# Four residual convolution layers on one NeuronCore: work between the layers in another order

## The chip, the cores and the metric

The kernel runs on one core of a Trainium2 chip. The metric is the device time of one execution in microseconds (us). The time of the kernel before is the median of three runs. Beside these runs there is one execution recorded by the hardware profiler; all times of single instructions, waits and transfers come from it.

## The reference, cut to what matters

The input x has the shape (4, 16, 512, 512) in float32: B = 4 images, C = 16 channels, 512 rows, 512 columns. Four layers follow each other, and each adds to x the result of a convolution of the normalised x:

```python
def _gn(v, G=8, eps=1e-5):          # GroupNorm: 8 groups of 2 channels, per image
    g = v.reshape(B_, G, C_ // G, H_, W_)
    m = jnp.mean(g, axis=(2, 3, 4), keepdims=True)
    s = jnp.var(g, axis=(2, 3, 4), keepdims=True)
    return ((g - m) / jnp.sqrt(s + eps)).reshape(v.shape)

x = x + L0(_gn(x)); x = x + L1(_gn(x)); x = x + L2(_gn(x)); x = x + L3(_gn(x))
```

- Layer 0 takes the 16 channels as 16 frames of a film. Two blocks come after each other. In a block each frame and its two neighbours go through three 5x5 convolutions with dilation 1, 2 and 4 and reflected edges; their results are weighted, added, and go through tanh.
- Layer 1 divides by the greatest absolute value of its whole input over 128, rounds to whole numbers between -127 and 127, runs a 3x3 convolution from 16 to 16 channels with zero edges, and scales the result and adds a bias.
- Layer 2 is the mean over a window of 17 rows and 17 columns, for each channel alone, with zero edges.
- Layer 3 takes the Fourier transform of each plane (rfftn over rows and columns), runs a complex 3x3 convolution from 16 to 16 channels over the frequencies, adds a complex bias, and transforms back.

A layer's normalisation needs the statistics of the whole image that the layer before put out (and layer 1 the greatest value of all images). So little of a layer can begin before the one before has ended.

## The kernel before, in words

All five engines take part. TensorE (PE) does the convolutions as matmuls into PSUM. ScalarE (ACT) and VectorE (DVE) normalise, round, add and gather statistics. SyncE (SP) issues nearly all transfers, ScalarE some at the beginning, and GpSimd (POOL) adds a few sums over the partitions. An engine works through its own instructions in order; one that has to wait holds up all that stand behind it. In the main loops the order is written out by hand: the program's order is each engine's order (`manual_schedule`).

**Layer 0** is the class Layer0 (L121 to L777). Its work is cut into groups of four frames, four groups for each block and image, 32 groups in all. Each group has six slots p = 0 to 5, in `run` (L722): a slot issues one sixth of the group's matmuls (`products`, L506), gathers the sixth before (`gather`, L529), prepares the frames of the group to come (`early`, `late`, `fetch`), and at last hands the slot's transfers to SP (`transfers`, L204), each tied to one of the slot's matmuls so that they spread over it. Group -1 has slots without matmuls, in which the first frames are made ready.

Ahead of that, `first` (L268) asks for the first HELD = 6 frames of image 0, two halves of 512 KB each. `weights` (L153) loads the table of all taps (`l0_t`, 1008 KB, on ScalarE's queue), weights and adds them on VectorE, stores them to DRAM from ScalarE's queue, and works out the two biases from two further small loads (L186 to L189). `load_weights` (L192) then loads the six sets of weights from there, in 24 transfers on ScalarE's queue. After that come the statistics of the six frames on VectorE (`frame_stats`, L257: four `bn_stats` for each frame, one `bn_aggr` for each pair) and `finish_stats` (L227), in which GpSimd adds over the partitions, and `rstd_bias` (L799) takes the square root on ScalarE and ends with the scale and the bias of the three groups. Only then can a frame be normalised (`x_frame`, L389; its rows at the edges, the rims, are loaded by `load_rims`, L345, and normalised at L366 to L382). The statistics of frames 6 to 15 are spread over the slots by `rest_of_first` (L291): one frame for each slot, two for each from (-1, 4) on. Their halves are loaded into the pool `x`, which has six buffers and is shared with the frames themselves. The sum of the other images' statistics is done in other slots.

**Layer 1** (L860) works through 64 chunks u of 8 rows of all four images. A chunk is loaded three chunks ahead, `rounded` normalises and rounds it (ScalarE, then VectorE) into one of three tiles `l1q`, which have a zero column at either end, `products` runs 256 matmuls, and `write` scales (ScalarE) and takes statistics (VectorE `bn_stats`, 64 x 6 values for each image). Before the first chunk, VectorE builds the weights `l_wt` from `l1_w` (a memset, L896, six operations, L901, and two scaled ones, L903) and clears the three `l1q` (L909). At the end four `bn_aggr` (L1007) put the statistics of 64 chunks together, one for each image, and `by_group` and `rstd_bias` turn them into scale and bias.

**Layer 2** (L1028) works through 64 planes i (image, channel). Each is loaded whole (1024 KB), normalised on ScalarE (L1070), multiplied twice with a band matrix (L1052), added to x (L1092) and stored. Every 16 planes `group_stats` (L827) ends an image's statistics. After image 1 and at layer 3's start, `edges` (L1255) works out in four steps, one for each step of layer 2's loop, what layer 3 needs of the images' first and last rows; it loads column sums that layer 2 stored.

`layer3_weights` (L1154) runs between layers 1 and 2: SP loads 14 constants, VectorE derives layer 3's weights (L1184 to L1231). Two more constants, band and cs, are loaded by layer 2.

**Layer 3** (L1347) works through 64 blocks yb of 8 rows. For a block: `load` (four transfers of 256 KB), `fold` (VectorE, sums and differences of the halves, L1253), `normal` (ScalarE, L1405), `products` (VectorE, L1421 and L1425), `rows` and `spread` (the block's own weights, VectorE then ScalarE), `imaginary` (L1456), `turned` (transposes, L1490), `scalars`, `real`, `hilbert` (L1515) and `write` (L1534). Before the loop the first two blocks are brought under way, together with the edges of images 2 and 3.

Of the kernel before, what the change touches and what calls it, by code (L numbers as in the profile page):

```python
# [20 lines left out]
P = 128  # L21
B, C, H, W = 4, 16, 512, 512
NYB = H // 8
G = 8
# [96 lines left out]
class Layer0:  # L121
# [31 lines left out]
    def weights(self):  # L153
# [28 lines left out]

        self.biases = k.const.tile([P, 2], F32, name="l0bias")
# [84 lines left out]
    def first(self):  # L268

        self.mv0 = self.k.stats.tile([P, G, 2], F32, name="xmv0")  # L270
        self.held = {}
        for t in range(HELD):
            fr = self.free.pop()
            raws = [fr[:, 2 * W * h : 2 * W * h + 2 * W] for h in range(2)]
            for h in range(2):
                self.load_half(raws[h], 0, t, h)
            self.held[0, t] = fr, raws
        self.weights()
        for q in ORDER:
            self.load_weights(0, q)  # L280
        for t in range(HELD):
            self.frame_stats(t, self.held[0, t][1])
        self.free.append(self.held.pop((0, HELD - 1))[0])
        self.finish_stats(0, self.mv0[:, 0 : HELD // 2])
        self.ahead = []
# [5 lines left out]
    def rest_of_first(self, n, p):  # L291

        if n == -1 and p == 0:
            self.transfers()
            for t in (HELD, HELD + 1):
                self.load_ahead(t)
            self.transfers()
        for _ in range(1 if n < 0 and p < 4 else 2):
            if self.ahead:
                t, raws = self.ahead.pop(0)  # L300
                self.frame_stats(t, raws)
                self.load_ahead(t + 2)
                if t == C - 1:
                    self.finish_stats(0, self.mv0[:, HELD // 2 : G], HELD // 2)
# [131 lines left out]
    def fetch(self, gr, p):  # L436

        b, conv, g = gr["b"], gr["conv"], gr["g"]
        if g == 0:
            order = {0: (1, 2), 1: (4,), 2: (3,), 4: (5,)} if conv else {0: (1,), 1: (2,), 2: (4,), 3: (3,), 4: (5,)}  # L440
        else:
            order = {0: (2,), 1: (4,), 2: (3,), 4: (5,)} if conv else {0: (2,), 1: (4,), 2: (3,), 4: (5,)}
        for i in order.get(p, ()):
            if g == 3 and i == 5:
                continue
            t = 4 * g - 1 + i
            if conv:
# [3 lines left out]
            rim = self.load_rims(b, t0) if i < 3 else None  # L451
            raws = None if (b, t) in self.held else [self.load_x(b, t, h, "xr") for h in range(2)]
            self.later(1, partial(self.made, gr, i, t, t0, rim, raws))
# [268 lines left out]
    def run(self):  # L722
# [57 lines left out]
class Kernel:  # L780
# [79 lines left out]
    def layer1(self, x1, x2, gn):  # L860
        tc, nc = self.tc, self.nc
        scale, bias, amax = gn
        with ExitStack() as ctx:
# [4 lines left out]
            wrep = self.load(wpool, "l1_w")  # L868
# [25 lines left out]

            wt = wpool.tile([P, 2, 4, 2, C], F32, name="l1_wt")
            nc.vector.memset(wt, 0.0)  # L896
            for a, yo, dhs in ((0, 0, (0, 1)), (0, 1, (None, 0)), (1, 0, (2, None)), (1, 1, (1, 2))):
                o = wt[:, a, 0:3, yo, :]
                for y, d in enumerate(dhs):
                    if d is not None:  # L900
                        nc.vector.scalar_tensor_tensor(o, wrep[:, d], row[:, y : y + 1], o, ALU.mult, ALU.add)  # L901
# [6 lines left out]
            for q in qs:  # L908
                nc.vector.memset(q, 0.0)  # L909
# [70 lines left out]
            with tc.tile_pool(name="l1ps", bufs=2, space=PSUM) as psum, tc.manual_schedule():  # L980
# [7 lines left out]
                for u in range(NYB + 2):  # L988
# [13 lines left out]
                    last = ps  # L1002

            gps = ctx.enter_context(tc.tile_pool(name="l1gps", bufs=2, space=PSUM))
            mv = wpool.tile([P, B, 2], F32, name="l1mv")
            for b in range(B):
                nc.vector.bn_aggr(mv[:, b, :], st[b].rearrange("p u s -> p (u s)"))  # L1007
# [20 lines left out]
    def layer2(self, x2, x3, sums, gn, l3):  # L1028
        tc, nc = self.tc, self.nc
        res, under_way = [], []  # L1030
        with ExitStack() as ctx:
# [10 lines left out]
            band = self.load(wpool, "c_band")  # L1042
            cs = self.load(wpool, "c_cs")
# [76 lines left out]
            with tc.manual_schedule():  # L1120
# [5 lines left out]
                for i in range(n + 1):  # L1126
# [11 lines left out]
                    if i > 0 and i % C == 0:  # L1138
                        b = i // C - 1
# [14 lines left out]
    def layer3_weights(self, wpool):  # L1154

        nc = self.nc
        l3 = SimpleNamespace(pool=wpool)
# [13 lines left out]
        bb = self.load(wpool, "l3_b")  # L1171

# [61 lines left out]
        return l3  # L1234
# [20 lines left out]
    def edges(self, l3, q, gn, sums, tiles, ps_u, ps_s):  # L1255
# [8 lines left out]
        yield 1  # L1264

# [81 lines left out]
    def layer3(self, x3, sums, gn, l3, out):  # L1347
# [3 lines left out]
        with ExitStack() as ctx:  # L1351
# [196 lines left out]
            with tc.manual_schedule():  # L1548
                edge = self.edges(l3, 1, gn, sums, tiles, ps_u, ps_s)
                next(edge)  # L1550
                for yb in range(2):
                    load(yb)
# [4 lines left out]
                next(edge)  # L1557
# [19 lines left out]
                turned(0)  # L1577
                next(edge, None)
                scalars(0)
# [25 lines left out]
    def run(self):  # L1605
# [5 lines left out]
        gn2 = self.layer1(x1, x2, gn1)  # L1611
        with self.tc.tile_pool(name="l3w", bufs=1) as wpool:
            l3 = self.layer3_weights(wpool)
            gn3 = self.layer2(x2, x3, sums, gn2, l3)
            self.layer3(x3, sums, gn3, l3, self.out)
# [63 lines left out]
```

## Time and profile before

| | us |
|---|---|
| median of 3 runs (5329.09 to 5343.41) | 5341.05 |
| profiled execution | 5351.83 |
| its span | 5350.0 |
| granted TensorE clock in it | 0.98 |
| TensorE busy with matmuls | 5027.4 (94%) |
| VectorE busy | 4035.8 (75%) |
| ScalarE busy | 2488.7 (47%) |
| mean DMA throughput | 161 GB/s |

The stages, by TensorE's matmuls in the trace:

| stage | us |
|---|---|
| start, to the first matmul of layer 0 | 0 to 80.8 |
| layer 0 | 80.8 to 3035.3 |
| layer 1, from its first full chunk | 3078.0 to 3666.7 |
| layer 2 | 3696.2 to about 4338 |
| layer 3, from its even running | 4384.0 to 5350 |

How to read it: the profile's span runs from the first to the last instruction, and the execution's own time is 1.8 us longer. Line numbers (L954) are those of the kernel shown here. Busy shares are means over stages of different kinds. An entry such as "DVE l1q L909" names the engine, the tile that is written, and the line; "SPq" and "ACTq" is an engine issuing a transfer. The chain of work follows back from the last instruction: at each step to what released it.

### The profile page before, as it was taken

The numbers are of one execution on the slowest core, as the hardware profiler recorded it, in microseconds if no ns is written. First come the engines' busy times: TensorE is split into PE (matmuls) and PEld (weight loads), VectorE is DVE, ScalarE is ACT, GpSimd is POOL, SyncE is SP. The second block draws the span as 40 slices with busy tenths as digits, with TensorE's granted clock in tenths as the row PEclk, the third lists the DMA queues.
The fourth block names the chain that finished last, engine by engine and source line by source line (L and its number), as shares of the span: only waits on it lengthen the run. The fifth ranks groups of instructions, "written<-read, shape, count | busy, mean of one in ns | idle before, by whom it ended". The sixth has DMA issues, their size and how long they took to land.

```text
span 5350.0 us, 270373 instructions
## 1 busy us (share of the span) xinstructions
PE 5027.4 (94%) x125040; PEld 3635.9 (68%) x125040; DVE 4035.8 (75%) x4739; ACT 2488.7 (47%) x3951; POOL 6.1 (0%) x18
## 2 busy tenths in 40 slices
PE   3999998999999999989999799997999979999999
PEld 2876676766666756757767565555887857777776
DVE  7867989768988669897688855555555578888887
ACT  2543345533245533443123454453454546666665
POOL 0000000000000000000000000000000000000000
PEclk9999999999999999999999899998999989999999
DMA  5455554555555455543345477775666655555554
GB/s 193 143 146 154 144 153 146 160 143 140 143 151 169 143 157 138 157 125 117 105 129 149 126 219 228 227 232 189 223 223 199 220 149 148 148 145 144 148 142 122
DMA packets 444349, 861.22 MB, mean 161 GB/s; under 512 B 73553, under 2 KB 95697, under 8 KB 442961
## 3 DMA queue, kind: packets, MB, share of 16 engines
q1 hardware_dynamic: 415216, 797.62, 51.1%
q10 hardware_dynamic: 28000, 46.31, 2.7%
q8 instruction: 979, 16.04, 1.4%
q14 instruction: 154, 1.25, 0.1%
HBM read 503.74 MB, written 339.90 MB: 158 GB/s over the span
## 4 chain that ended last, share of the span: by engine, by line
PE 90%; DVE 5%; issue 2%; DMA 1%; ACT 1%; SPq 0%; ACTq 0%; DVEq 0%; POOL 0%
PE m L518 53%; PE l1p L957 10%; PE l2p L1052 7%; PE u L1515 5%; PE s L1456 4%; PE u L1456 4%; PE u L1478 2%; PE pt L1490 2%; DVE l2o L1092 2%; PE l2p L1103 1%; DVE st L1093 1%; PE pr L1500 0%; DVE xst L264 0%; DVE frame L434 0%; DVE xb L625 0%
## 5 line engine op out<-in xcount | busy, mean ns | idle before, releaser
L518 PE MATMUL m<-frame,l0w 32*32 32x512 f32 x86016 | 2869.2, 605 | 166.1 <-DVE frame L474 80.8
L518 PEld LDWEIGHTS m<-frame,l0w 32*32 32x32 f32 x86016 | 2060.0, 103 | 974.4 <-issue 374.0
L434 DVE SCALAR_TENSOR_TENSOR frame<-frame,frame 128x2376 f32<-128x2376 f32 x232 | 607.8, 2628 | 8.3 <-DMA xb<-in_x 0.3
L957 PE MATMUL l1p<-l1q,l_wt 32*32 32x512 f32 x12288 | 484.4, 601 | 71.0 <-DVE l1q L947 38.4
L957 PEld LDWEIGHTS l1p<-l1q,l_wt 32*32 32x32 f32 x12288 | 259.5, 103 | 241.1 <-issue 164.7
L1092 DVE TENSOR_TENSOR l2o<-l2x,l2p 128x512 f32<-128x512 f32 x256 | 172.8, 675 | 258.7 <-PE l2p L1052 258.7
L645 ACT ACTIVATE junk<-xb,neg 128x1024 f32<-128x1024 f32 x256 | 294.3, 1150 | 63.8 <-DMA l0w<-l0w 31.3
L1052 PEld LDWEIGHTS l2p<-k_c_band,l2y 128*128 128x128 f32 x2048 | 256.7, 190 | 75.4 <-issue 54.6
L1052 PE MATMUL l2p<-k_c_band,l2n 128*128 128x144 f32 (+1 forms) x2048 | 271.4, 293 | 25.2 <-ACT l2n L1070 17.4
L1052 PE MATMUL l2p<-k_c_band,l2y 128*128 128x144 f32 (+1 forms) x2048 | 284.2, 292 | 6.1
L1081 ACT COPY l2y<-l2p 128x512 f32<-128x512 f32 x256 | 150.0, 586 | 285.1 <-PE l2p L1052 285.1
L1052 PEld LDWEIGHTS l2p<-k_c_band,l2n 128*128 128x128 f32 x2048 | 264.9, 198 | 25.8 <-ACT l2n L1070 17.8
L974 DVE BATCH_NORM_STATS2 l1st<-l1o 128x6 f32<-128x512 f32 x256 | 158.3, 681 | 161.9 <-ACT l1o L972 161.9
L972 ACT ACTIVATE l1o<-l1p,k_l_bias,l_osc 128x1024 f32<-128x1024 f32 x128 | 147.3, 1201 | 249.3 <-PE l1p L957 243.4
L1515 PE MATMUL u<-k_c_hil,zt 128*128 128x128 f32 x2048 | 255.9, 278 | 0.0
L551 ACT COPY C<-m 128x1024 f32<-128x1024 f32 x64 | 61.6, 1014 | 393.6 <-PE m L518 312.7
L1515 PEld LDWEIGHTS u<-k_c_hil,zt 128*128 128x128 f32 x2048 | 238.4, 192 | 2.1 <-issue 0.8
L398 DVE STREAM_TRANSPOSE frame<-xp 128x1056 f32<-128x1056 f32 x128 | 162.7, 1281 | 101.6 <-ACT xp L372 101.6
L1491 ACT COPY zt<-pt 128x512 f32<-128x512 f32 x256 | 131.5, 600 | 211.4 <-PE pt L1490 211.4
L1421 DVE TENSOR_TENSOR xc<-l3n,k_c_tab 128x2048 f32<-128x2048 f32 x64 | 146.7, 2293 | 108.3 <-ACT l3n L1405 108.3
L1534 DVE SCALAR_TENSOR_TENSOR l3o<-u,l3t 128x256 f32<-128x256 f32 x512 | 192.2, 427 | 23.7 <-ACT l3t L1526 20.9
L957 PE MATMUL l1p<-l1x,l_wt 32*32 32x512 f32 x4088 | 197.8, 597 | 0.0
(303 smaller groups left out, 6372.3 us busy)
## 6 DMA issues: line engine op xcount, KB each, us to landing
y<-y SPq DMA_DIRECT2D x256, 264.0 KB
frame<-y SPq DMA_DIRECT2D x512, 132.0 KB
x<-l1o SPq DMA_DIRECT2D x256, 256.0 KB
l2x<-x SPq DMA_DIRECT2D x64, 1024.0 KB
x<-l2o SPq DMA_DIRECT2D x64, 1024.0 KB
l3x<-x SPq DMA_DIRECT2D x256, 256.0 KB
out<-l3o SPq DMA_DIRECT2D x256, 256.0 KB
l1x<-x SPq DMA_DIRECT2D x252, 256.0 KB
```

What stands on the lines that cost most here:

```text
L398: nc.vector.transpose(v[:, :, 4 + h : 68 : 2], xp)
L434: self.nc.vector.scalar_tensor_tensor(o, x, f, y, ALU.mult, ALU.add)
L518: ins = nc.tensor.matmul(ps[PX * j : PX * j + PX, i, :].rearrange("p (k r) -> p k r", r=64), w[rows, n], v[rows, k0 : k0 + 8, r0 : r0 + 64 ...
L645: nc.scalar.activation(junk, xs[h], f, bias=neg, accum_out=self.out_sums[n][:, 2 * t + h : 2 * t + h + 1])
L957: ins = nc.tensor.matmul(ps[32 * j : 32 * j + 32, b, :], wt[rows, a, d], qs[v % 3][rows, k, d : d + W] if d < 3 else raws[v][rows, k], sta ...
L974: nc.vector.bn_stats(st[b][:, u, :], o[:, b, :])
L1052: nc.tensor.matmul(ps[:, lo:hi], lhs[:, k, at : at + P], band[:, j : j + hi - lo], start=(k == 0), stop=(k == 3), skip_group_check=True,)
L1081: nc.scalar.copy(yts[i][:, wb, :], ps)
L1092: nc.vector.tensor_add(o[:, hb, :], xt[:, hb, :], ps)
L1456: nc.tensor.matmul(ps[b][32 * j : 32 * j + 32], f[rows, n, j, :], x[rows, j, :], start=(i == 0), stop=(i == 2 and tag == "s"), skip_group_ ...
L1515: nc.tensor.matmul(po[:, bass.ts(k, P)], zt[:, b, k ^ 1, :], hil[:, k, :], start=False, stop=(k == 3), skip_group_check=True,)
L1534: nc.vector.scalar_tensor_tensor(o[:, v].rearrange("p k u -> p u k"), po[:, HW:W].rearrange("p (u k) -> p u k", u=2), s, t.rearrange("p (u ...
```

## The change: what it does

In the beginning of layer 0:
- The weights of layer 1, as far as they don't depend on data, are built first of all (`layer1_weights`, on tiles of layer 0 that are still free) and stored to DRAM; layer 1 loads them.
- The statistics of frames 0 and 1 come ahead of `weights`, those of frames 2 to 5 after it and after the 24 weight loads are issued.
- The biases become a function of their own, `take_biases`, called in slot (-1, 3).
- The rims of the first frames are asked for ahead of the statistics.
- The statistics of frames 6 to 15 move to later slots: two frames in slots (-1, 5) and (0, 0), then one in each; `finish_stats` runs for them in two parts, once for groups 2 to 4 (frames 4 to 9) and once for groups 5 to 7 (frames 10 to 15), instead of once for groups 3 to 7; groups 0 to 2 are done at the start as before.

In layer 1: only the two edge columns of the `l1q` tiles are cleared; layer 3's constants are loaded at chunk 4 and its weights derived at chunk 12 (`layer3_weights` becomes a generator in a pool opened ahead of layer 1, and takes over band and cs); the statistics of chunks 0 to 59 are put together at chunk 61, those of the last four at the end, and joined by five small operations.

In layer 2: `group_stats` of an image runs one plane later; `edges` of images 0 and 1 yields once more between its loads and their use.

In layer 3: before the loop, the first block's rows are loaded ahead of the edges' sums, and its fold, normalisation, products and matmuls come ahead of the edges' steps and of the second block.

```diff
@@ first
+        self.k.layer1_weights(self.free[3])
+        for t in range(2):
+            self.frame_stats(t, self.held[0, t][1])
         self.weights()
         for q in ORDER:
             self.load_weights(0, q)
-        for t in range(HELD):
+        self.rims_ahead = {t0: self.load_rims(0, t0) for t0 in (0, 1)}
+        for t in range(2, HELD):
             self.frame_stats(t, self.held[0, t][1])
@@ rest_of_first
-        if n == -1 and p == 0:
-            self.transfers()
+        if (n, p) == (-1, 0):
             for t in (HELD, HELD + 1):
                 self.load_ahead(t)
-            self.transfers()
-        for _ in range(1 if n < 0 and p < 4 else 2):
+        if (n, p) == (-1, 3):
+            self.take_biases()
+        for _ in range(2 if (n, p) in ((-1, 5), (0, 0)) else 1 if n >= 0 else 0):
             if self.ahead:
                 t, raws = self.ahead.pop(0)
                 self.frame_stats(t, raws)
                 self.load_ahead(t + 2)
-                if t == C - 1:
-                    self.finish_stats(0, self.mv0[:, HELD // 2 : G], HELD // 2)
+                for lo, hi in ((2, 5), (5, G)):
+                    if t == 2 * hi - 1:
+                        self.finish_stats(0, self.mv0[:, lo:hi], lo)
@@ run
-                    if g < 1:
+                    if g < 2:
                         self.rest_of_first(g, p)
@@ new
+    def layer1_weights(self, t):
+        nc = self.nc
+        self.l1_wt = scratch(self.dram, "l1_wt", [P, 2, 4, 2, C])
+        w = t[:, 0 : 9 * C].rearrange("p (h d c) -> p h d c", h=3, d=3)
+        row = t[:, 9 * C : 9 * C + 2]
+        wt = t[:, 256 : 256 + 16 * C].rearrange("p (a n y c) -> p a n y c", a=2, n=4, y=2)
+        nc.scalar.dma_start(w, self.a["l1_w"])
+        nc.scalar.dma_start(row, self.a["c_pair"])
+        nc.vector.memset(wt, 0.0)
+        for a, yo, dhs in ((0, 0, (0, 1)), (0, 1, (None, 0)), (1, 0, (2, None)), (1, 1, (1, 2))):
...
+        nc.scalar.dma_start(self.l1_wt, wt)
@@ layer1
             for q in qs:
-                nc.vector.memset(q, 0.0)
+                nc.vector.memset(q[:, :, 0 :: W + 1], 0.0)
+            mv4 = wpool.tile([P, 2, B, 2], F32, name="l1mv4")
...
+                    if u in (4, 12):
+                        ahead()
+                    if u == NYB - 3:
+                        for b in range(B):
+                            nc.vector.bn_aggr(mv4[:, 0, b, :], st[b][:, 0 : NYB - 4].rearrange("p u s -> p (u s)"))
...
-                nc.vector.bn_aggr(mv[:, b, :], st[b].rearrange("p u s -> p (u s)"))
+                nc.vector.bn_aggr(mv4[:, 1, b, :], st[b][:, NYB - 4 : NYB].rearrange("p u s -> p (u s)"))
+            part = 4.0 / NYB
+            t = self.small.tile([P, B, 2], F32, name="l1mvt", tag="l1mvt")
+            nc.vector.tensor_scalar_mul(t, mv4[:, 1], part)
+            nc.vector.scalar_tensor_tensor(mv, mv4[:, 0], 1.0 - part, t, ALU.mult, ALU.add)
+            d = self.small.tile([P, B], F32, name="l1mvd", tag="l1mvd")
+            nc.vector.tensor_sub(d, mv4[:, 0, :, 0], mv4[:, 1, :, 0])
+            nc.vector.tensor_mul(d, d, d)
+            nc.vector.scalar_tensor_tensor(mv[:, :, 1], d, part * (1.0 - part), mv[:, :, 1], ALU.mult, ALU.add)
@@ layer2
-                    if i > 0 and i % C == 0:
-                        b = i // C - 1
+                    if i > C and i % C == 1 or i == n:
+                        b = (i - 1) // C - (i < n)
@@ edges
         yield 1
+        if q == 0:
+            yield 1
@@ layer3
+                load(0)
                 edge = self.edges(l3, 1, gn, sums, tiles, ps_u, ps_s)
                 next(edge)
-                for yb in range(2):
-                    load(yb)
...
-                next(edge)
+                fold(0)
+                load(1)
+                normal(0)
...
-                for yb in range(2):
-                    rows(yb)
-                    spread(yb)
-                    fold(yb)
-                    load(yb + 2)
-                    normal(yb)
-                    next(edge, None)
-                    products(yb)
-                    masked(yb)
-                    next(edge, None)
+                rows(0)
+                spread(0)
+                products(0)
+                imaginary(0)
+                load(2)
+                masked(0)
+                next(edge)
+                fold(1)
+                turned(0)
+                load(3)
+                normal(1)
+                rows(1)
+                spread(1)
+                next(edge)
+                scalars(0)
+                products(1)
+                next(edge)
+                masked(1)
+                next(edge, None)
                 fold(2)
-                imaginary(0)
-                turned(0)
-                next(edge, None)
-                scalars(0)
```

More of the change, by code (lines that the diff above doesn't have):

```diff
@@ L181, in weights, with take_biases @@
             nc.scalar.dma_start(to[half], wq[2 * PX * half : 2 * PX * half + 2 * PX])
+    def take_biases(self):
+        k, nc = self.k, self.nc
         self.biases = k.const.tile([P, 2], F32, name="l0bias")
@@ L450, in fetch @@
             t0 = 0 if i == 1 else min(4 * g + 1, 12)
-            rim = self.load_rims(b, t0) if i < 3 else None
+            rim = (self.rims_ahead.pop(t0, None) or self.load_rims(b, t0)) if i < 3 else None
             raws = None if (b, t) in self.held else [self.load_x(b, t, h, "xr") for h in range(2)]
@@ L853, in layer0, with layer1 @@
             return Layer0(self, ctx, x1).run()
-    def layer1(self, x1, x2, gn):
+    def layer1_weights(self, t):
[8 more added lines that the diff above has]
+        for a, yo, dhs in ((0, 0, (0, 1)), (0, 1, (None, 0)), (1, 0, (2, None)), (1, 1, (1, 2))):
+            o = wt[:, a, 0:3, yo, :]
+            for y, d in enumerate(dhs):
+                if d is not None:
+                    nc.vector.scalar_tensor_tensor(o, w[:, d], row[:, y : y + 1], o, ALU.mult, ALU.add)
+        nc.scalar.dma_start(self.l1_wt, wt)
+    def layer1(self, x1, x2, gn, ahead):
         tc, nc = self.tc, self.nc
@@ L866, in layer1 @@
             work = ctx.enter_context(tc.tile_pool(name="l1work", bufs=2))
-            wrep = self.load(wpool, "l1_w")
+            wt = wpool.tile([P, 2, 4, 2, C], F32, name="l1_wt")
+            nc.sync.dma_start(wt, self.l1_wt)
             wsc = self.load(wpool, "l1_scale")
@@ L892, in layer1 @@
             nc.vector.tensor_scalar_mul(back, row, back[:, 0:1])
[L895 to L901, printed above, removed]
             for a in range(2):
@@ L1041, in layer2 @@
             nc.vector.memset(pc, 0.0)
-            band = self.load(wpool, "c_band")
-            cs = self.load(wpool, "c_cs")
+            band, cs = l3.band, l3.cs
             mv = wpool.tile([P, B, G, 2], F32, name="mv3")
@@ L1156, in layer3_weights @@
         nc = self.nc
-        l3 = SimpleNamespace(pool=wpool)
+        l3 = self.l3 = SimpleNamespace(pool=wpool)
+        l3.band = self.load(wpool, "c_band")
+        l3.cs = self.load(wpool, "c_cs")
         l3.hil = self.load(wpool, "c_hil")
@@ L1233, in layer3_weights @@
         l3.cor = wpool.tile([P, B // 2, W], F32, name="cor")
-        return l3
+        yield 2
     def own(self, gn, images, name):
@@ L1264, in edges @@
         yield 1
+        if q == 0:
+            yield 1
         nc.vector.tensor_add(two[:, 0:2], xt[:, 0:2], xt[:, 2:4])
@@ L1610, in run @@
         gn1 = self.layer0(x1)
-        gn2 = self.layer1(x1, x2, gn1)
         with self.tc.tile_pool(name="l3w", bufs=1) as wpool:
-            l3 = self.layer3_weights(wpool)
-            gn3 = self.layer2(x2, x3, sums, gn2, l3)
-            self.layer3(x3, sums, gn3, l3, self.out)
+            steps = self.layer3_weights(wpool)
+            gn2 = self.layer1(x1, x2, gn1, partial(next, steps))
+            gn3 = self.layer2(x2, x3, sums, gn2, self.l3)
+            self.layer3(x3, sums, gn3, self.l3, self.out)
 @with_exitstack
```

## The prediction

> **What bounds the kernel now.** I began with the chain that ended last, on the profile's page, because it says where the span can be shortened at all.
>
> ```profile
> PE 90%; DVE 5%; issue 2%; DMA 1%; ACT 1%; SPq 0%; ACTq 0%; DVEq 0%; POOL 0%
> ```
>
> TensorE's matmuls carry 90% of the span and the change takes no matmul away. So only the 10% in which TensorE waits can pay. The view of busy time by stretches finds them. Of its eight stretches, four are the joints between stages (columns: stretch, PE, PEld, DVE, ACT, POOL busy, clock, DMA share, GB/s).
>
> ```profile
> 0.00:81.00 81.00, 0.18 (x16) 0.18 (x32) 55.71 (x102) 21.35 (x48) 1.25 (x7) 1.00 0.64 220
> 3034.00:3078.00 44.00, 3.16 (x37) 0.47 (x16) 37.80 (x80) 24.35 (x36) 1.49 (x3) 0.56 0.66 189
> 3667.00:3697.00 30.00, 2.07 (x7) 1.83 (x8) 20.53 (x79) 4.45 (x4) 0.00 (x0) 0.56 0.63 216
> 4338.00:4384.00 46.00, 19.75 (x200) 12.50 (x200) 33.41 (x75) 13.66 (x22) 0.00 (x0) 0.74 0.68 140
> ```
>
> TensorE is busy 0.2 of 81 us, 3.2 of 44, 2.1 of 30 and 19.8 of 46: about 176 us idle in all, most of what TensorE lacks (5350.0 - 5027.4 = 323, the rest being short gaps in the slots). Each part of the change sits at one of these joints, so I price them one by one, from the chain inside each. The profiled execution took 5351.83 us (span 5350.0 and 1.83 around it), 10.8 above the median of 5341.05; savings are read from the one and taken off the other.
>
> **The beginning (0 to 80.8).**
>
> ```profile
> 14.06 9.41 DMA l0p<-in_l_par
> ...
> 24.75 4.77 DVE xst L264 x8
> ...
> 44.20 1.07 DVE xst L264 x2
> 45.27 0.04 issue
> 45.31 1.27 DVE xst L264 x2
> ```
>
> Before, VectorE waits 10.8 us for the biases (l0p, from 12.7 to 23.5) with the statistics of six frames queued behind (three pairs of 4.7 + 0.4). The change takes the two frames' statistics ahead of the weights and puts the biases off to slot (-1, 3). Worked out: layer 1's weights cost one small load, a memset and six operations of 0.24 (the L901 row of layer 1), done by about 4.3 us. The load of l0_t (1.18, landing 6.86) sits behind their store on ScalarE's queue, so it is issued near 5.3 and lands near 11, while VectorE is at frames 0 and 1, which are done by 12.6; the weights' 5.8 us end at 18.4 instead of 12.75; the two remaining pairs end at about 28.5 instead of 40.1. That looks like 11 us. I don't count it, for this row of ScalarE's timeline:
>
> ```profile
> 23.38 16.05 ACTq L194 DMA_DIRECT2D l0w<-l0w  x24
> 39.45 1.28 ACT L805 ACT_TABLE_LOAD   x1 [39.45 <-DMA rim<-in_x]
> 42.59 0.20 ACT L805 ACTIVATE s_x<-v_x 128x3 f32<-128x3 f32 x1 [1.85 <-DVE v_x L803]
> ```
>
> The square root s_x stands on ScalarE behind 24 weight loads, which begin when the weights' store has landed (23.3). That store now leaves 5.6 us later, but with the x loads (last at about 23 to 28) nearly out of its way: landing about 25. 16.05 more is 41.4, the table load 42.7; s_x at 42.7, by which the scales come at 44.1, as before. Here the Trainium skill ("DMA: Bandwidth & Descriptors", Issuing engines are not separate DMA queues) says otherwise: issuing costs only the sequencer's time, usually small. 24 loads at the 0.43 of one issue are about 11.3 us with the gaps between them, so the queue would be free 4.8 us earlier and the start with it. The row shows 16.05, because an issue waits for an earlier DMA's completion. I take the row; by the page's price it would be 5 more.
>
> What does pay is behind the scales. The two statistics between scales and first frame (1.07 + 1.27 above) go: 2.4. The rims were issued by SP from 46.6 to 53.3 after them, and ScalarE's xp_r waited 4.9 for the loads; they are now asked for long before, so xp_r's second part comes at about 49.7 instead of 57.0: 7.3 including the 2.4. Statistics at 62.8 and 70.2 (2.5 and 2.8) leave the chain too, 5.3; the biases' wait and operations come in, about 1.3 + 1.1. Sum 7.3 + 5.3 - 2.4 = 10.2. **First matmul near 70.5, gain 10** (5 if l0_t or the store lands late, 20 if the queue does not hold).
>
> **The first slots.** The statistics of frames 6 to 15 (2.4 each) now lie in slots (-1, 5) to (1, 0), their loads in pieces. VectorE is 81% busy in this stage (2386 of 2953), a slot of 14.7 leaves it 2.8: one frame per slot just fits, two at (-1, 5) and (0, 0) don't. But before had two per slot as well and lost 3.65 at 128. Net +1, between -8 (a stall while six x buffers are held) and +4.
>
> **Layer 0 to 1 (3034 to 3078).**
>
> ```profile
> 3041.68 1.77 DVE l1q L909
> ...
> 3061.99 1.77 DVE l1q L909
> ```
>
> VectorE is the chain. Three memsets over 2056 columns go: 5.3, and 1.1 of issue before them; the six weight operations take 0.8 of the chain and the tile's memset 0.3; a row's memset of 0.48 moves ahead. Three tiny memsets come in. That makes 6.9 to 7.3 for VectorE, but ScalarE's last squares (5.4 us per frame) would then be late: they lose a wait of 3.6 for the weights' load, and end about 4.5 to 5 earlier. First l1x load at 58.5 instead of 64.4. **Gain 6** (3 to 7.5).
>
> **Inside layer 1.** At u = 4 SP gets 16 constant loads (0.43 each, 7.5 us), with loads three chunks ahead and DMA at 0.73; at u = 12 VectorE gets layer 3's weights, 10.1 us as measured after layer 1, against 4.2 us of slack in a chunk of 9.1; at u = 61 four aggregates of 60 chunks (6.7). All lie beside TensorE, which has two buffers of lead. If cover is gone, each costs what goes beyond it, up to 5.9 for the weights. **-1** (0 to -6).
>
> **Layer 1 to 2 (3667 to 3697).**
>
> ```profile
> L1007 DVE BATCH_NORM_AGGREGATE l1mv<-l1st 128x2 f32<-128x384 f32 x4 | 7.1, 1840 | 0.0
> ```
> ```profile
> 3687.99 5.64 DMA l2x<-x
> ```
>
> Two parts. The aggregate runs over four chunks of statistics, 24 values instead of 384: by its nearest row (0.37 for 48 values) 1.4, and five small operations of 0.2 join the halves: 2.4 for 7.1, so bias_x comes 4.7 earlier, at 3679.1 for 3683.8. And SP no longer issues 16 constants from 3680.7 to 3688 in front of the first l2x load. The load itself needs the memory that layer 1 gives back, which VectorE's last reader frees, about 3675.4 after the change; 5.6 of landing makes 3681, ScalarE's l2n 2.1 more, with TensorE at 3683 for 3696.17. l2x and bias_x then come within 2 us of each other: the later sets it. **Gain 13** (7 to 15).
>
> **Inside layer 2.** The statistics of an image move one step later; the three gaps of 2.2 + 0.9 stay. The edge of q = 0 gets one more step before it is used:
>
> ```profile
> PE l2p L1052 <- ACT l2y L1081: 7.8, 1, 7.8
> ```
>
> 3.2 of the 7.8 is VectorE waiting for l2edge_x, and one step (some 9 us) covers it. 3.2 less 1.2 for statistics that now share a step: **+2** (0 to 3).
>
> **Layer 2 to 3 (4338 to 4384).**
>
> ```profile
> 4342.92 4.90 DMA l3edge_x<-sums
> 4347.84 8.43 DMA l3x<-x
> ```
>
> SP issued eight edge loads (4341.6 to 4345.2) before the first rows; now the rows go first. Landing: 4341.7, four issues, and 6.5 to 8.5 to land = 4350 for 4356.3. From there VectorE has the same operations: fold 2.4, normalise (ScalarE) 2.4, products and reduces 6.8 + 0.3, edge additions 3.3 (they were done in the wait before), fold 2.4, row and edge products 3.0 beside ScalarE's second normalisation, products 6.8: 27.4, and the third fold (2.3), which stood in front of the scalar row, comes after. 27.7 before, so the landing's 6.3 is kept, and part of the 2.3. **Gain 7** (3 to 10).
>
> **Sum.** 10 + 1 + 6 - 1 + 13 + 2 + 7 = 38: the profiled execution would be 5314, the median 5341 - 38 = **5303**.
>
> **The rivals.** *The start pays in full*: ScalarE's loads do not hold s_x, since the store lands early or the loads pass faster. 11 more: 5292. For it: the x loads are over by then, and the DMA share falls. Against: the 16.05. *The next wait takes over*: at each joint something stands close behind the removed wait: ScalarE's squares, the release of layer 1's memory, the stores of layer 2 that share the queues with l3x. With 5 at the start, 3, 8 and 3 at the joints, and -1 inside: 18, 5323. *The joints are not on the path as told*, or what is gained is given back within the stage: 5341. Against: TensorE idles in each, and each stage after is bound by TensorE. *Slower*: one mechanism, in slots (-1, 5) to (1, 0). An xs load that waits for one of the six x buffers, freed by VectorE's statistics late in a slot, stands at the head of SP's queue, with the next frames' loads behind it; TensorE then misses the frame and a slot of 14.7 us is lost. Five of the eight slots would be 73, less 38: 5376. It decides from three lost slots (44 over 38). For it: six buffers, four taken from the start. Against: before, the same six buffers served the same loads and the largest gap there was 3.65.
>
> **Chances.** The sum as told 0.60; start in full 0.15; next wait takes over 0.17; nothing kept 0.04; slower 0.04. The range reaches from the start in full with good joints, 5284, to the poor joints with a little more, 5328. About 0.3% (16 us) is what can be told from no change: faster by more 0.88 (0.60 + 0.15 + most of 0.17), within 0.07, slower 0.05.
>
> **What would show it.** In the profile after: first matmul at about 70.5, and ScalarE's s_x just after its 24th load and the table load (if s_x comes by 33, the first rival is right); layer 1's first full chunk 6 us sooner after layer 0's last matmul (44 to 38); layer 2's first matmul 16 us after layer 1's last (29 before); layer 3's even running about 39 us after layer 2's end (46 before); gaps in slots 0 to 6 no longer than 4; no gap over 3 at layer 1's 4th and 12th chunk. The forecast would be wrong by most if l2x still waits for something after bias_x, or if slots 0 to 6 open gaps.

## The result, and the profile after

The changed kernel takes 5332.65 us (median of 22 runs, 5314.9 to 5342.99), the kernel before 5344.3 in the same comparison (22 runs). The ratio is 0.9975, with a 95% interval of 0.9967 to 0.9983: 0.25% faster, some 13 us (9 to 18), where 38 were forecast. The time lies above the range of the prediction, which ended at 5328.

The profiled execution of the changed kernel took 5314.9, as forecast for it (5314). That agreement is an accident: it is the fastest of the 22 runs, and the profiled execution of the kernel before, 5351.8, was one of its slower ones. A second profile of the kernel before, before_again, spans 5305.2 us instead of 5350.0, with each of its four joints within 2 us of the first. It was taken on another occasion, on which the kernel's median was 5316. So two profiles can't be subtracted as wholes. What can be compared is each joint, and the slots and gaps inside a stage.

From the page, the chain that ended last, of the changed kernel:

```profile
PE 89%; DVE 6%; issue 2%; DMA 2%; ACT 1%; SPq 0%; ACTq 0%; POOL 0%; DVEq 0%; POOLq 0%
```

It has hardly moved from TensorE's 90%. The stretches of the changed kernel that answer to the four joints (columns as before: stretch, PE, PEld, DVE, ACT, POOL busy, clock, DMA share, GB/s):

```profile
0.00:74.00 74.00, 0.00 (x0) 0.00 (x0) 47.34 (x90) 21.35 (x48) 1.25 (x7) 1.00 0.57 187
...
3027.00:3065.00 38.00, 1.88 (x2) 0.17 (x2) 30.39 (x72) 24.55 (x35) 1.48 (x3) 0.54 0.81 223
...
3646.00:3662.00 16.00, 1.47 (x6) 1.00 (x4) 7.32 (x32) 4.47 (x4) 0.00 (x0) 0.65 0.84 297
...
4304.00:4347.00 43.00, 21.86 (x276) 14.08 (x291) 32.52 (x76) 13.16 (x21) 0.00 (x0) 0.68 0.69 151
```

All four are shorter: first matmul at 74.4 instead of 80.8, layer 0 to 1 39.0 instead of 42.7, layer 1 to 2 16.0 instead of 29.4, layer 2 to the first product of layer 3's loop 43.2 instead of 50.0. That is 30 us. The stages between them say how much of it lasts. The table counts from TensorE's matmuls; a slot is 448 of layer 0's matmuls, and slot 12 begins its third group. The columns before and after are one occasion; before_again, again and again_2 were run on three chips.

| | before | before_again | after | again | again_2 |
|---|---|---|---|---|---|
| first matmul | 80.8 | 82.8 | 74.4 | 74.8 | 74.3 |
| slot 8 begins | 206.0 | 207.0 | 198.8 | 199.6 | 198.3 |
| slot 12 begins | 263.0 | 264.2 | 263.9 | 265.0 | 264.0 |
| layer 0 to 1 | 42.7 | 42.9 | 39.0 | 39.0 | 39.4 |
| layer 1 | 588.7 | 576.0 | 580.7 | 584.2 | 567.1 |
| layer 1 to 2 | 29.4 | 29.3 | 16.0 | 15.8 | 15.7 |
| layer 2's matmuls | 641.8 | 636.0 | 641.7 | 638.9 | 636.2 |
| end of layer 2's matmuls to the end | 1012.1 | 1011.4 | 1009.1 | 1009.7 | 1009.5 |
| span | 5350.0 | 5305.2 | 5313.1 | 5312.0 | 5286.3 |

The lead of 6 to 8 at the first matmul is still there at slot 8 and gone at slot 12. In layer 3 the joint is 7 shorter, but of that only 2 to 3 are left at the end. Layer 1's length differs by up to 17 us between profiles of one and the same kernel, so no edit can be read from it.

### The profile page after: what moved, and what is told of

It reads as the page before. It is cut to its first block, busy times and chain, and to the rows that moved or that the text cites. A ratio compares the mean times of both kernels' runs of the same rounds, so it can differ in the third digit from the quotient of the medians.

```text
span 5313.1 us, 270477 instructions
## 1 busy us (share of the span) xinstructions
PE 5014.8 (94%) x125040; PEld 3651.4 (69%) x125040; DVE 4034.6 (76%) x4764; ACT 2491.1 (47%) x3954; POOL 6.8 (0%) x20
## 4 chain that ended last, share of the span: by engine, by line
PE 89%; DVE 6%; issue 2%; DMA 2%; ACT 1%; SPq 0%; ACTq 0%; POOL 0%; DVEq 0%; POOLq 0%
PE m L525 51%; PE l1p L975 10%; PE l2p L1082 8%; PE u L1550 4%; PE s L1491 4%; PE u L1491 4%; PE u L1513 2%; PE pt L1525 2%; DVE l2o L1122 2%; PE l2p L1133 1%; DVE st L1123 1%; DVE frame L441 0%; PE pr L1535 0%; ACT xp L377 0%; DVE zr L627 0%
## 5 line engine op out<-in xcount | busy, mean ns | idle before, releaser
L525 PE MATMUL m<-frame,l0w 32*32 32x512 f32 x86016 | 2856.1, 604 | 170.5 <-DVE frame L481 74.4
L1082 PE MATMUL l2p<-k_c_band,l2n 128*128 128x144 f32 (+1 forms) x2048 | 272.5, 294 | 14.4 <-ACT l2n L1100 10.9
## 6 DMA issues: line engine op xcount, KB each, us to landing
y<-y SPq DMA_DIRECT2D x256, 264.0 KB
```

The lines of the kernel that those rows point to most:

```text
L525: ins = nc.tensor.matmul(ps[PX * j : PX * j + PX, i, :].rearrange("p (k r) -> p k r", r=64), w[rows, n], v[rows, k0 : k0 + 8, r0 : r0 + 64 ...
L1082: nc.tensor.matmul(ps[:, lo:hi], lhs[:, k, at : at + P], band[:, j : j + hi - lo], start=(k == 0), stop=(k == 3), skip_group_check=True,)
```

## The experiments

Ratios are to the kernel before on the same chip (its medians there were 5316 to 5324). On one chip each: again, old_start, old_l3_start and weights_between; before_again, image1_later, stats_as_before and three_mended; aggregates_only, joint3_only, again_2 and mended_2; start_only and old_start_fold.

**again**: the changed kernel, unedited.

> The changed kernel once more, unedited, for a second profile of it. Its one profiled execution so far took 5314.9, 18 below the median of 5332.65, and that of the kernel before 5351.8, 7 above its median; so the profiles differ by 37 and the medians by 12. Theory 1 (given back inside the stages): the joints are as short as in the first profile (first matmul at 74.4, layer 0 to 1 in 39.0, layer 1 to 2 in 16.0, layer 2 to layer 3's first real product in 43.2, each within 1.5), and a stage between them is longer by some 15 us in all than in the first profile, layer 1 (580.7) or layer 0 (2952.2) most likely. Theory 2 (the joints themselves vary): joints are 10 us or more longer in sum, and the stages are as before within 5.

Ratio 0.9966 (0.9954 to 0.9978); the joints as in the table, layer 0 2949.6 and layer 1 584.2. The joints repeat within 1.5, as theory 1 says, so theory 2 is out. But no stage is 15 longer than in the first profile either, so this run doesn't show where the gain is given back.

**old_start**: the old beginning in the changed kernel, layer 1's weights built in layer 1.

```diff
-        self.k.layer1_weights(self.free[3])
-        for t in range(2):
-            self.frame_stats(t, self.held[0, t][1])
         self.weights()
...
-        self.rims_ahead = {t0: self.load_rims(0, t0) for t0 in (0, 1)}
-        for t in range(2, HELD):
+        for t in range(HELD):
...
-        for _ in range(2 if (n, p) in ((-1, 5), (0, 0)) else 1 if n >= 0 else 0):
+        for _ in range(1 if n < 0 and p < 4 else 2):
```

(cut; the biases too go back to their old place)

> The changed kernel with the beginning of the kernel before (statistics after the weights, biases in front, rims late, frames 6 to 15 as before, layer 1's weights built in layer 1). If the start's gain of 6.4 in the profiles (80.8 to 74.4) reaches the end: 6 to 8 slower than the changed kernel, ratio to before about 0.9988; first matmul at 80.8. If the moved statistics cost in the slots what the start gained (gaps over 0.3 us in layer 0 were 93 after and 81 before): no slower than the changed kernel, ratio about 0.9975, and layer 0 shorter by 6 or more.

Ratio 0.9954 (0.9942 to 0.9966): not slower than again on the same chip (0.9966), but if anything faster. First matmul at 82.7. The beginning of each slot against again: 7.9 later at slot 0, 8.7 later at slot 8, 0.4 later at slot 12. In the slots 4 to 11 it has no gap at all, again has 7.4 us of them. The second expectation holds: what the beginning gains goes in the slots. Layer 0 to 1 took 37.0 here, 2 less than with layer 1's weights built ahead (39.0).

**old_l3_start**: the old order at the start of layer 3.

> The changed kernel with the order of the kernel before at the start of layer 3. If layer 3's joint is worth its 6.8 in the profiles: layer 2 to layer 3's first real product in 50 instead of 43, 7 slower, ratio to before about 0.9988. If it is given back in layer 3's loop (which took 965.9 after that, and 962.1 before): loop near 962, 3 slower at most, ratio about 0.998.

Ratio 0.9975 (0.9964 to 0.9986), beside again's 0.9966: 5 slower, but the intervals overlap. The profile is sharper: the joint took 50.2 and the rest 960.9, together 1011.1 against 1009.1 to 1009.7 with the new order. So the order is worth about 2, not 7.

**weights_between**: both steps of layer 3's weights called after layer 1.

```diff
-                    if u in (4, 12):
-                        ahead()
...
             gn2 = self.layer1(x1, x2, gn1, partial(next, steps))
+            for _ in range(2):
+                next(steps)
```

> The changed kernel with layer 3's constants and weights back between layers 1 and 2 instead of at chunks 4 and 12 of layer 1. If their place ahead is worth what the profile shows: layer 1 to 2 in 24 instead of 16, 8 slower, ratio to before about 0.999. If the 16 loads and VectorE's 10 us of weights cost inside layer 1 as much: layer 1 shorter by 5 to 10, total unchanged within 3, ratio about 0.9975.

Ratio 0.9967 (0.9955 to 0.9979). It didn't test what it was made for. Outside the loops that are written out the instructions are ordered anew, and the trace has the loads and the weights ahead of layer 1, not behind it: layer 0 to 1 took 51.0 and layer 1 to 2 stayed at 15.8. It shows what they cost where TensorE waits for them: 12 us.

**before_again**: the kernel before, a second profile.

> The kernel before once more, unedited, for a second profile. First profile: first matmul 80.8, layer 0 2954.5 long, layer 0 to 1 42.7, layer 1 588.7, layer 1 to 2 29.4, layer 2 641.8, to layer 3's first real product 50.0, the rest 962.1. If the joints are fixed and the stages' lengths are the chip's: joints within 1.5 of these, layer 1 anywhere between 575 and 590. If layer 1 is longer in the changed kernel because of the constants and weights put into it: layer 1 here near 575, below the 576 to 584 that three profiles of the changed kernel's layer 1 showed.

The joints are as in the first profile within 2 (table above), layer 1 576.0. That layer 1 grew by the constants put into it can't be seen: 567 to 584 with them, 576 to 589 without.

**image1_later**: image 1's statistics out of group 0's slots.

```diff
-        if cur and cur["conv"] == 0 and cur["b"] + 1 < B and p >= 2:
-            self.input_stats(cur["b"] + 1, 4 * cur["g"] + p - 2)
+        if cur and cur["conv"] == 0 and cur["b"] + 1 < B:
+            at = 6 * cur["g"] + p - 8 if cur["b"] == 0 else 4 * cur["g"] + p - 2 if p >= 2 else -1
+            if at >= 0:
+                self.input_stats(cur["b"] + 1, at)
```

> The changed kernel with image 1's statistics (their loads too) moved from slots (0, 2) on, four in a group, to slots (1, 2) on, one in each slot, so that they don't lie beside those of image 0. Theory 1 (the transfers of two images meet at SP): the 10 us that are lost against the old start between slots 8 and 10 of layer 0 shrink to 3 or less, slot 12 comes 6 to 8 earlier than with the old start, layer 0 shorter by about as much, and the whole is 6 faster than the changed kernel. Theory 2 (VectorE's work up to there is the bound, and an earlier first matmul only waits longer): still even with the old start by slot 10 to 12 within 2, total unchanged.

Slot 12 began at 254.2, 10.0 earlier than in before_again on the same chip: theory 1. Next, waits of TensorE (between 85 and 240 us) and of SP (between 110 and 225 us) (columns: waiting engine and line, for whom: us in all, times, longest), first in the kernel before:

```profile
PE m L518 <- issue: 3.7, 1, 3.7
```
```profile
SPq L209 <- PE m L518: 61.7, 67, 5.5
```

in the changed kernel:

```profile
PE m L525 <- DVE frame L441: 5.7, 2, 4.4
```
```profile
SPq L211 <- PE m L525: 25.1, 34, 6.2
SPq L211 <- DVE xst L266: 15.5, 3, 7.9
```

and in image1_later:

```profile
PE m L525 <- DVE frame L441: 0.2, 1, 0.2
```
```profile
SPq L211 <- PE m L525: 34.5, 48, 3.0
SPq L211 <- DVE xst L266: 22.2, 3, 9.0
```

SP's wait for the statistics is new with the change, and it is there in image1_later too, even longer. What differs is what stands behind it. SP's timeline of the changed kernel (start, us, what, how many):

```profile
159.88 3.84 SPq L211 DMA_DIRECT2D xr<-in_x  x8
163.82 15.48 SPq L211 DMA_DIRECT2D xs<-in_x  x24
179.35 2.91 SPq L211 DMA_DIRECT2D y<-y  x4
182.36 6.82 SPq L211 DMA_DIRECT2D rim<-in_x  x10
```

and of image1_later:

```profile
159.50 3.57 SPq L211 DMA_DIRECT2D xs<-in_x  x8
163.18 2.93 SPq L211 DMA_DIRECT2D y<-y  x4
169.45 6.81 SPq L211 DMA_DIRECT2D rim<-in_x  x10
```

Ahead of the first stores of y stand 24 pieces of xs here and 8 there. With them the stores leave SP at 179 instead of 163. ScalarE then waits for them before it may write y again:

```profile
ACT y L600 <- DMA y<-y: 8.7, 1, 8.7
ACT L600 <- DMA y<-y: 3.8, 1, 3.8
```

(changed kernel, 170 to 220 us; no such wait in image1_later between 150 and 225). VectorE waits for ScalarE, the frame comes late, and TensorE stands. The edit moved image 1's loads and ScalarE's work on them together; that the loads are what counts is read from these waits.

But the whole was only at 0.9971 (0.9959 to 0.9983), like the changed kernel. The lead over before_again was 10.9 at slot 19, 4.9 at slot 21 and 3.1 at slot 22, in the first block's last group; gaps of 4.2 and 1.5 us stand in front of the last two. In the trace the larger one has the same look. SP in image1_later:

```profile
342.21 24.94 SPq L211 DMA_DIRECT2D frame<-y  x32
367.60 4.49 SPq L211 DMA_DIRECT2D xs<-in_x  x8
372.19 3.01 SPq L211 DMA_DIRECT2D y<-y  x4
```

and in before_again:

```profile
353.28 24.50 SPq L209 DMA_DIRECT2D frame<-y  x32
377.88 1.80 SPq L209 DMA_DIRECT2D y<-y  x4
```

The edit has put eight pieces of image 1, 4.5 us, in front of these stores as well. ScalarE waits for the stores, and TensorE for the frame that comes after (image1_later, 375 to 393 us):

```profile
ACT y L600 <- DMA y<-y: 15.9, 1, 15.9
PE m L525 <- DVE frame L441: 4.2, 1, 4.2
```

In before_again ScalarE waits 9.6 there and TensorE doesn't wait for a frame.

**stats_as_before**: the new beginning, frames 6 to 15 in the old slots.

> The changed kernel's beginning up to the first slots, with the statistics of frames 6 to 15 back in the slots where the kernel before has them (one in each of (-1, 0) to (-1, 3), then two). Theory 1: first matmul 3 to 5 later than in the changed kernel (near 78 to 79), no loss between slots 8 and 10, and slot 12 about 3 to 4 earlier than with the old start (265.3). Theory 2 (VectorE's total is the bound): slot 12 within 1.5 of 265.

Ratio 0.9979 (0.997 to 0.9988). First matmul at 87.7, later than with either beginning, and slot 12 at 268.0, 3.8 later than before_again. Neither theory foresaw that; no run separates its cause. It does show that no stall opens in slots 4 to 12 with the old placing (0.0 us of gaps).

**three_mended**: the table of taps asked for first, image 1's statistics later, layer 3's fold of block 2 earlier.

```diff
+        self.load_taps()
         self.k.layer1_weights(self.free[3])
...
                 scalars(0)
+                fold(2)
                 products(1)
...
-                fold(2)
```

> The changed kernel with three edits: the load of the table of taps issued before layer 1's weights, image 1's statistics later as in image1_later, and layer 3's fold of block 2 ahead of the products of block 1. Expected: first matmul 6 to 9 earlier than 74.4 (the table took 12.2 us in the profile after, and 5.7 where it was issued first); if SP's meeting of two images is the loss, slot 12 about 10 to 14 earlier than with the old start, else no more than 2; layer 3's block 1 no longer 3 to 4 longer than before, 3 off the end. In all 15 faster than the changed kernel by theory 1, 4 by theory 2.

Ratio 0.9952 (0.994 to 0.9964). First matmul at 71.3, 3 earlier, not 6 to 9; slot 12 12.7 earlier than in before_again; and the lead fell again, from 13.0 at slot 19 to 5.7 at slot 22. The first block of layer 3's loop took 14.5, as in the kernel before (14.7), instead of 17.4 to 18.5, which shows where the joint's gain goes in the changed kernel. VectorE in the changed kernel:

```profile
4345.52 2.35 DVE L1286 TENSOR_TENSOR l3d<-l3x 128x1024 f32<-128x1024 f32 x2
4350.97 2.29 DVE L1456 TENSOR_TENSOR xc<-l3n,k_c_tab 128x2048 f32<-128x2048 f32 x1 [3.11 <-ACT l3n L1440]
```

and in three_mended:

```profile
4315.06 2.35 DVE L1293 TENSOR_TENSOR l3d<-l3x 128x1024 f32<-128x1024 f32 x2
4317.32 2.29 DVE L1463 TENSOR_TENSOR xc<-l3n,k_c_tab 128x2048 f32<-128x2048 f32 x1
...
4328.35 2.29 DVE L1463 TENSOR_TENSOR xc<-l3n,k_c_tab 128x2048 f32<-128x2048 f32 x1 [2.04 <-ACT l3n L1447]
```

In the changed kernel the fold of block 2 comes last (4345.5), ScalarE can normalise only after it, and VectorE waits 3.1; block 2's products are late and TensorE waits twice (1.3 for its weights f, 0.8 for rr). With the fold ahead of block 1's products ScalarE works beside them.

**aggregates_only** and **joint3_only**: parts of the layer 1 to 2 joint in the kernel before. The first splits the statistics; the second also moves constants and weights into layer 1 (with band and cs).

> The kernel before with one edit: layer 1's statistics put together in two parts (60 chunks inside the loop, four at the end). By the prediction's working the layer 1 to 2 joint shortens by 4.7 from 29.4, to 24.7, since both the weights' loads and the scale hang on the same chain; ratio to before 0.9991. If the joint's loads are bound by something else: 29 still.

> The kernel before with the edits of the layer 1 to 2 joint alone: statistics in two parts, and layer 3's constants and weights at chunks 4 and 12 of layer 1. The joint's profile will be 16.0 as in the changed kernel. If what a joint saves reaches the end of the kernel: 13.4 less, ratio 0.9975; joint layer 0 to 1 unchanged at 42.8, layer 3's start 50.0. If the constants and weights in layer 1 cost as much as they save: ratio 0.999 to 1.0 and layer 1 longer than in aggregates_only by 6 or more.

The joint took 23.2 with the first (29.4 before) and 16.1 with the second; ratios 0.999 (0.998 to 1.0001) and 0.998 (0.9973 to 0.9988), that is 5 us (0 to 11) and 11 us (6 to 14). So of the 13.3 in the joint some 11 reach the end, and at least 6. Between chunks 3 and 8 of layer 1 joint3_only fell 5 behind aggregates_only, with two gaps of 1.6 and 1.7 there. That may be a part of the price of the constants; no run separates it. In the three profiles of the changed kernel chunk 8 came 0 to 2 later, measured the same way against the kernel before.

**again_2**: the changed kernel on another chip.

> The changed kernel unedited, for a narrower interval of its gain on a second occasion: by the joints of its profiles against those of the kernel before (start 0, layer 0 to 1 3.8, layer 1 to 2 13.4, layer 2's edge 2.4, layer 3 3) it should be 21 to 23 faster, ratio 0.996, if the stages are as long as before; 12 to 13, ratio 0.9975, if they grew by 8 to 10.

Ratio 0.9972 (0.9962 to 0.9981): 15 us (10 to 20). The three comparisons, 0.9975, 0.9966 and 0.9972, agree.

**mended_2**: as three_mended, image 1's statistics two slots earlier.

> three_mended with image 1's statistics two slots earlier, (1, 0) to (3, 3), so that none lies in the last two slots of the first block, where image1_later and three_mended lost 7 at slot 22. If that was the loads of image 1 beside those of the second block's first frames: slot 24 about 12 earlier than in the kernel before (three_mended: about 6), whole 5 faster than three_mended, ratio 0.994. If not: no loss less, ratio 0.9952 as three_mended.

Ratio 0.9957 (0.9942 to 0.9972). The lead over before_again was 11.0 at slot 19 and 5.7 at slot 21: the same loss, so it isn't the loads of the last two slots. But eight pieces of image 1 still stand for 4.8 us in front of the same stores of y (SP, at 367.3), ScalarE waits 14.4 for them and TensorE 4.1 for the frame. So this run left in place what the traces point to. No run kept the head start of image1_later and took these pieces away; the cause of this loss is read from the traces, not shown.

**start_only**: the new beginning alone in the kernel before, without layer 1's weights.

> The kernel before with the new beginning alone (statistics of frames 0 and 1 ahead of the weights, biases in slot (-1, 3), rims ahead, frames 6 to 15 later), without layer 1's weights in front. First matmul at 68 to 72 instead of 82 (the table of taps is issued first again). If what the beginning gains is lost where image 0's and image 1's loads meet: gaps of 5 to 8 in slots 4 to 12, slot 12 within 2 of the kernel before's (263 to 265), the whole within 0.1% of the kernel before or slower. If the beginning's gain survived: slot 12 near 253, ratio 0.998.

Ratio 1.0004 (0.9992 to 1.0016). First matmul at 71.3; 10.9 ahead of before_again at slot 8, 3.6 at slot 10 and 3.5 at slot 12; gaps of 1.7 and 3.6 in front of slots 8 and 9. Slot 12 was to come within 2; otherwise it is as expected. The beginning gives the whole nothing that can be told: at most 4 us by the interval.

**old_start_fold**: old_start with the earlier fold.

> The changed kernel with the beginning of the kernel before (as old_start), and with layer 3's fold of block 2 ahead of the products of block 1. Expected: layer 3's block 1 not 3 to 4 longer any more, so 3 to 4 faster than old_start (0.9954): ratio 0.995, and as fast as the kernels with the new beginning mended (0.9952 and 0.9957). If the beginning is worth its 8 after all, 0.996 to 0.997.

Ratio 0.9955 (0.994 to 0.9969), as old_start (0.9954), not 3 to 4 faster; that size is below the interval. The profile has the fold's part: layer 3's first blocks as long as in the kernel before, and no gap over 0.3 in its loop.

The fastest ratios are those of three_mended, old_start, old_start_fold and mended_2, 0.9952 to 0.9957: better than the changed kernel by about 9 us. On the two chips that ran one of them beside the unedited changed kernel (old_start and again, mended_2 and again_2) the intervals overlap.

## Why the prediction was wrong, step by step

**The beginning, "gain 10", and "the first slots: net +1".** Here the forecast failed. The first half of the mechanism was seen: s_x came straight after the 24th load and the table load, so the weights' queue on ScalarE did bind. ScalarE's timeline of the changed kernel:

```profile
29.14 14.32 ACTq L196 DMA_DIRECT2D l0w<-l0w  x24
43.50 1.28 ACT L812 ACT_TABLE_LOAD   x1 [43.50 <-DMA l0w<-l0w]
44.80 0.20 ACT L812 ACTIVATE s_x<-v_x 128x3 f32<-128x3 f32 x1
```

The table of taps was mis-sized: I took the 5.68 of its old place.

```profile
5.72 12.20 DMA frame<-in_l_t
```
```profile
18.03 0.57 DVE L163 TENSOR_SCALAR frame<-frame,l0par 128x672 f32<-128x672 f32 x1 [4.11 <-DMA frame<-in_l_t]
```

Issued 4.5 us later than before, when loads of x had been going out on SP's queue since 2.1, it took 12.2, and VectorE waited 4.1 for it. The weights' store left at 23.8 and had landed at 29.1, not 25. The 24 loads then held ScalarE for 14.3: less than the 16.05 of the row that I carried over, more than the 11.3 by the page's price. The section cited there speaks of the sequencer's time alone and not of an issue that has to wait, so it didn't contradict the row. (And 25 and 16.05 are 41.05, not 41.4.) So s_x came at 44.8, 2.1 later than forecast. From s_x to the first matmul it took 29.6 instead of the 27.8 that my sum needs; the other 1.8 are there. First matmul 74.4 for 70.5: that cost 4. With the table asked for first (three_mended) 3 of them came back.

The larger error was the slots. I put them between -8 and +4 and took +1 by counting VectorE's work; they cost 7 to 8. The mechanism is the one I gave to the slower rival, a load waiting for an x buffer at the head of SP's queue, but with another end: what waited behind was not the next frames' loads, of which a slot of 14.7 would have been lost each time, but the stores of y, and the price was once 8 instead of five times 14.7. I had looked at image 0's loads and not at image 1's, which the kernel issues in slots (0, 2) to (0, 5), just where the change puts image 0's. image1_later shows that the two together are the loss: with image 1's moved away, slot 12 came 10 sooner. And start_only says what is left of the new beginning in the whole: 1.0004.

**Layer 0 to 1, "gain 6".** 3.5 to 4. VectorE lost its memsets as worked out, and ScalarE's last squares were indeed the next bound. But the term "they lose a wait of 3.6 for the weights' load, and end about 4.5 to 5 earlier" failed. ScalarE before and after:

```profile
3045.33 1.15 ACT L645 ACTIVATE junk<-xb,neg 128x1024 f32<-128x1024 f32 x1 [3.56 <-DMA k_l_w<-in_l_w]
```
```profile
3038.20 1.15 ACT L652 ACTIVATE junk<-xb,neg 128x1024 f32<-128x1024 f32 x1 [4.86 <-DMA k_l_bias<-in_l_bias]
```

The wait stayed and got longer; what ends it the profiles of the changed kernel put down to different loads, so that is open. Counted from layer 0's last matmul the squares ended at 26.3 for 25.3 before: 1 later. VectorE, no longer at its memsets, summed them at once (26.3 for 29.0), and from there to layer 1's first full chunk it took 12.7 for 13.7. With layer 1's weights built in layer 1 as before (old_start, old_start_fold) the squares ended at 24.1 and the joint took 37.0: a gain of 6 without that edit. Building the weights ahead took 2 of it, if the old beginning of these two kernels has no part in it some 2900 us later.

**Inside layer 1, "-1".** Right in order of size, as far as can be told: up to chunk 8 it is 0 to 2 in the changed kernel and 5 in joint3_only, in a stage whose length varies by 17.

**Layer 1 to 2, "gain 13".** Right: 13.4, by both parts. The aggregates of four chunks cost less than estimated:

```profile
L1030 DVE BATCH_NORM_AGGREGATE l1mv<-l1st 128x2 f32<-128x24 f32 x4 | 0.6, 214 | 0.0
```
```profile
3653.91 5.84 DMA l2x<-x
```

0.6 for 1.4. l2x is issued with nothing in front and lands in 5.8; the load and not the scale ends the joint. aggregates_only gave 6.2 for the 4.7 worked out.

**Inside layer 2, "+2".** The wait for the edge is shorter, as forecast, 3.4 for 7.8, but the three statistics cost more. Waits of TensorE, before and after:

```profile
PE ps_m L822 <- DVE mp_x L831: 6.6, 3, 2.2
```
```profile
PE l2p L1082 <- ACT l2y L1111: 3.4, 1, 3.4
PE ps_m L829 <- DVE mp_x L838: 7.7, 3, 2.6
```

A plane takes 9.3 us from its first matmul to the next plane's, in every profile, so the steps that differ can be counted. The edge's step went from 19.4 to 16.9 (15.7 in again_2); the three steps with statistics went from 45 to 46 together to 48 to 50. From the second plane's first matmul to the last plane's it took 612 and 610 in the two profiles before, and 613, 613 and 610 in the three of the changed kernel. So about 0: the step that failed is "less 1.2 for statistics that now share a step". Those 1.2 came out at 2 to 5 and took all that the edge gained; why they cost more is not shown.

**Layer 2 to 3, "gain 7".** The joint gained 6.8, the layer 2 to 3. The step that failed is "the third fold, which stood in front of the scalar row, comes after": I booked it as a saving, without asking who needs block 2's fold. Block 2's products were late, and the loop's first block longer by the 3 to 4 that three_mended gave back.

**The sum.** 0 for the beginning and slots, 3.7, 0 to -2, 13.4, 0, and 2 to 3: 17 to 20 by the traces, where 38 were forecast. The times say 13 (9 to 18), 18 (12 to 25) and 15 (10 to 20), which leaves nothing clear over. Of the missing 20, 11 are the beginning with its slots, and 2, 2 and 4 to 5 the joint to layer 1, layer 2 and layer 3. Of the rivals, "the next wait takes over" came nearest in size (-18). It fits the joint to layer 1, but not the joint to layer 2 that it named with 8; at the beginning and in layer 3 the gain was given back inside the stage, as the rival at 5341 has it. The first rival is excluded: s_x did not come by 33.

## What to carry to other kernels

A head start at the beginning is worth what it still is ten slots later: follow the slots' start times of both kernels side by side until they run parallel, before booking a gain. When work is moved to other slots, list everything that already sits in those slots on each queue, including other loops' loads that draw on the same pool, and ask what stands behind the first that must wait. When an operation moves behind a joint, ask who needs its result next; and where two profiles of one kernel differ by 45 us, compare joints and gaps, not spans.

## What the runs showed of the hardware

Two profiles of the kernel before, taken on two occasions, spanned 5350.0 and 5305.2 us with the same granted clock (0.98): layer 0's 86016 matmuls had TensorE busy for 2868.7 us in one and 2843.2 in the other, and layer 1 took 588.7 and 576.0. The joints agreed within 2 us. A load of 1008 KB, the same in both kernels, took 5.7 us when it was issued at 1.2 us, ahead of the x loads on the other queue (6 MB, from 2.1 us on), and 12.2 us when it was issued at 5.7 us, in the midst of them.
